# Spreading the first list over layer 0, and pulling rows ahead of pairs in the second product of a four-layer graph network

## Chip, cores and metric

The kernel runs on one NeuronCore of one Trainium2 chip. The metric is the device time of one execution in microseconds (us). In the text PE is TensorE, DVE is VectorE, ACT is ScalarE, POOL is GpSimd and SP is SyncE.

## What is computed

x is 4096 x 128. adj is 4096 x 4096, symmetric in its pattern, with some 0.2% of entries above zero and a full diagonal. There are four layers, each ending in a layer norm of x plus the layer's output.

```python
# layer 0: signed graph attention with the same matrix as mask and weight
hw = x @ W;  scores = where(adj > 0, e_plus[None, :], NEG_INF)
x = layernorm(x + softmax(scores) * adj @ hw)
# layer 1: Chebyshev convolution of order 3, twice (hidden width 256)
Tx1 = L @ x;  Tx2 = 2 * (L @ Tx1) - x
h = elu(x @ W0[0] + Tx1 @ W0[1] + Tx2 @ W0[2] + b0)      # then once more with W1, b1
x = layernorm(x + elu(...))
# layers 2 and 3: attention with four heads, and a mean over neighbours
```

Here L is adj. The change touches layer 0 and the first three of layer 1's four products with L.

## The kernel before

**Dense part.** adj is read from memory as transposed chunks of 512 x 512 in f32 (1 MB each). `chunk` (L145) sends them on SP's queue into a pool of five buffers. There are NB = 8 blocks of IB = 512 rows, each of TB = 4 tiles of 128. A dense product with L goes block by block: for each of 8 chunks `propagate` issues four f32 matmuls into `pacc` (L714), calls a hook `seen`, and at the end of the block the second product forms `t2T` on VectorE (L762), multiplies by W1A (L769), applies ELU (two `hT` on VectorE, L704), and goes on with the next block.

**Sparse part.** Later layers, and part of layer 1, use lists of the entries of each row instead of dense products. For a list, `take` finds in each row of a chunk the 8 largest values and their places (MAX8 and FIND_INDEX8, L1359 and L1360: one pair a row of 128x512). `build(c)` makes list c out of the finds in three steps: the first ends in a `count` (L1386) and, four times over, a chain of MAX8 and MATCH_REPLACE8 (L1398, L1400); the second takes a small matmul with `count` (L1410) and makes `spread` (L1418, L1419); the third takes matmuls with `spread` (L1434) and makes `both_at` (L1462) for lists 0 to 2, or `where` (L1476) for the others. `first_list` (L365) does the takes of list 0 in layer 0.

**Gathers.** GpSimd gathers rows by list with indirect DMAs, each followed by a one-element operation as a pause (L1480, L1526). `pairs(c)` is 36 gathers of both directions of list c's entries (`both_ways`), which need `both_at`. A pull is nine gathers of 128 rows for one unit, that is one tile of 128 rows. In the second product blocks 0 and 1 are done by lists, as units 0 to 7: `pull(u)` gathers, `weigh(u)` makes three `hot` matrices (L1514) and adds six weighed rows to `here` (L1517), and `product(u)` multiplies on TensorE (L1587, L1589). In the third product blocks 0 to 2 are done so, as units 0 to 11 with two buffers for the rows, beside list 3 to 7's building.

**What sets the order.** In layers 0 and 1 a scheduler places the instructions on each engine by its own estimate of when they are ready. `keep_in_program_order` ties an instruction behind the one before it on its engine in the program's text, and to no other. Each engine works through its instructions in the order so fixed. In the second product the plan of hooks (0 to 47, one a chunk) gives the order of the text. Chunks 4 to 7 of a block are FAR: their takes are made in the second product. From the fourth product on the order is written by hand.

In layer 0 the loop goes over i (row block) and n (column chunk); `pos` (L329) makes masks on VectorE, L398 adds up edge sums, L410 the products, `count_bad` (L382) checks each chunk on ScalarE.

Of the kernel before, what the change touches and what calls it, by code (L numbers as in the profile page):

```python
# [11 lines left out]
F32 = mybir.dt.float32  # L12
# [9 lines left out]
P = 128  # L22
# [24 lines left out]
def adj_resnorm_d4(ctx: ExitStack, tc: tile.TileContext, x_in, xT_in, adj, adjT, pairs, diag_in, w0g, w0gT, a0, w1a, b1a,  # L47
# [234 lines left out]
    def layer0(ld, ps_acc, ps_tr, ps_mm):  # L282
# [9 lines left out]
        with tc.tile_pool(name="l0", bufs=1) as l0, tc.tile_pool(name="l0w", bufs=2) as l0w, \  # L292
# [74 lines left out]

            def first_list(i, a):
                top, at = firsts
                for k in range(TB):  # L370
                    row = a[:, k, :]
                    if i == 0:
                        row = x[:, k * TB:(k + 1) * TB, :].rearrange("p t f -> p (t f)")
                        nc.scalar.copy(row, a[:, k, :])
                        d = row[:, k * P:(k + 1) * P]
                        nc.vector.scalar_tensor_tensor(d, ident, less_own[0][:, k:k + 1], d, op0=ALU.mult, op1=ALU.add)
                    nc.vector.max(top[:, k, i, :], row)
                    nc.vector.max_index(at[:, k, i, :], top[:, k, i, :], row)

# [79 lines left out]
            for i in range(2):  # L459
# [5 lines left out]
                for n, j in enumerate(order):  # L465
# [14 lines left out]
                    if j == 0:  # L480
                        first_list(i, a)
                    if n == 1 and rest:
                        diagonal_product(*rest)
                        diagonal_sums(*rest)
# [15 lines left out]
            def sums_of(i, j, pe, first, last, pool=ld, name="chunk"):  # L500
                a = chunk(pool, adjT, i, j, name, True)
                pos = masks(a)
                edge_sums(pe, pos, j, both, first, last)
                count_bad(a, i * NB + j)
                if j == 0:
                    first_list(i, a)
                return j, a, pos
# [5 lines left out]
            for i in range(2, NB):  # L513
# [55 lines left out]
                if i == 5:  # L569
                    tc.keep_in_program_order(nc.sync.dma_start(x, x_in.rearrange("(t p) f -> p t f", p=P)))  # L570
# [91 lines left out]
    degrees, firsts, less_own = [], [], []  # L662

    def network(usual):

        with ExitStack() as whole:
# [3 lines left out]
            with ExitStack() as first, ExitStack() as l1h_pool:  # L670
                ps_acc, ps_tr, ps_mm = [first.enter_context(tc.tile_pool(name=n, bufs=2, space=PSUM, reuse_waits="tile"))
                                        for n in ("ps_acc", "ps_tr", "ps_mm")]
                if usual:
# [4 lines left out]
                    less_own[:] = [early.tile([P, NT], F32, name="less_own")]  # L678
                    nc.scalar.dma_start(own_entries, diag_in)
                    nc.vector.tensor_scalar_mul(less_own[0], own_entries, -1.0)  # L680
# [102 lines left out]
                for ib, blk, p in propagate(lambda jt: t1[:, jt, :], seen=second, blocks=[b for b in range(NB) if not usual or b not in LAST]):  # L783
# [506 lines left out]

    class Lists:
# [3 lines left out]
        def __init__(self, whole, first, layer, own_entries):  # L1295
# [9 lines left out]
            self.diag = own_entries  # L1305
            self.source = keep.tile([P, NT, NEAR + QT], I32, name="source")
# [42 lines left out]
        def take(self, ib, c, a, pinned=False):  # L1349
            pin = tc.keep_in_program_order if pinned else lambda r: r  # L1350
            for k in range(TB):
                t = c * TB + k
                row = a[:, k, :]
                if ib == c:
# [3 lines left out]
                    pin(nc.vector.scalar_tensor_tensor(d, ident, less_own[0][:, t:t + 1], d, op0=ALU.mult, op1=ALU.add))  # L1358
# [3 lines left out]
        def indices(self, out, key):  # L1362

            miss = self.work.tile([P, key.shape[1], key.shape[2]], F32, name=f"miss{key.shape[2]}", bufs=1)
            nc.vector.tensor_scalar(miss, key, 0.0, float(N + 1), op0=ALU.is_le, op1=ALU.mult)
            nc.vector.scalar_tensor_tensor(out, key, -1.0, miss, op0=ALU.add, op1=ALU.add)

        def build(self, c, pinned=False):
            pin = tc.keep_in_program_order if pinned else lambda r: r
            work = self.work  # L1370
# [11 lines left out]
            nc.vector.tensor_scalar(flat(there), flat(top), 0.0, None, op0=ALU.is_gt)  # L1382
            nc.vector.tensor_reduce(deg, rows(there), AX.X, ALU.add)
            nc.vector.tensor_reduce(self.bad[:, 2, c:c + 1], deg, AX.X, ALU.max)
            nc.vector.tensor_scalar(deg, deg, float(-NEAR), 0.0, op0=ALU.add, op1=ALU.max)
            nc.vector.tensor_copy(count, deg)  # L1386
            nc.vector.tensor_copy(flat(key), flat(found_at))
            nc.vector.tensor_tensor(rows(key), rows(key), self.first.rearrange("p s r -> p (s r)")[:, None, :].to_broadcast([P, TB, NB * 8]), ALU.add)
            nc.vector.tensor_mul(flat(key), flat(key), flat(there))
            pairs = top.rearrange("p k s r -> p (k s) r")  # L1390
            nc.vector.tensor_reduce(self.bad[:, 0, c:c + 1], pairs[:, :, 7], AX.X, ALU.max)
            nc.vector.tensor_tensor(twice, pairs[:, :, 0:7], pairs[:, :, 1:8], ALU.is_equal)
            nc.vector.tensor_mul(twice, twice, pairs[:, :, 1:8])
            nc.vector.tensor_reduce(self.bad[:, 1, c:c + 1], twice, AX.XY, ALU.max)
            for k in range(TB):
                row, left = rows(key)[:, k], rows(there)[:, k]
                for n in range(0, MOST, 8):
                    nc.vector.max(best[:, k, n:n + 8], row if n == 0 else left)  # L1398
                    if n + 8 < MOST:
                        nc.vector.match_replace(left, best[:, k, n:n + 8], row if n == 0 else left, -1.0)  # L1400
            nc.vector.tensor_copy(rec[:, :, 0:REST], best[:, :, NEAR:MOST])
            nc.vector.tensor_sub(best[:, :, NEAR:MOST], best[:, :, NEAR:MOST], rec[:, :, 0:REST])
            nc.vector.tensor_copy(rec[:, :, REST:2 * REST], best[:, :, NEAR:MOST])
            nc.vector.tensor_copy(rec[:, :, 2 * REST], self.own.to_broadcast([P, TB]))
# [6 lines left out]
            nc.vector.tensor_copy(base, pb)  # L1411
            nc.vector.tensor_tensor(end, base, deg, ALU.add)
            nc.vector.tensor_copy(rec[:, :, 2 * REST + 1], base)
            nc.vector.tensor_tensor(deg, base, rec[:, :, 2 * REST + 1], ALU.subtract)
            nc.vector.tensor_copy(rec[:, :, 2 * REST + 2], deg)
            at = work.tile([P, TB, SLOTS], BF16, name="spread")
            for k in range(TB):
                nc.vector.tensor_scalar(at[:, k], self.slot, base[:, k:k + 1], None, op0=ALU.is_ge)  # L1418
                nc.vector.scalar_tensor_tensor(at[:, k], self.slot, end[:, k:k + 1], at[:, k], op0=ALU.is_lt, op1=ALU.mult)  # L1419
            nc.scalar.dma_start(self.spread[c], at.rearrange("p k s -> p (k s)"))  # L1420
            nc.vector.tensor_reduce(self.bad[:, 3, c:c + 1], end, AX.X, ALU.max)
            for k in range(TB if c not in PAIRED else 0):
                same = work.tile([P, NEAR, NB * 8], F32, name="same", bufs=1)
                nc.vector.tensor_tensor(same, best[:, k, 0:NEAR][:, :, None].to_broadcast([P, NEAR, NB * 8]),
                                        rows(key)[:, k][:, None, :].to_broadcast([P, NEAR, NB * 8]), ALU.is_equal)
                nc.vector.tensor_tensor(same, same, rows(top)[:, k][:, None, :].to_broadcast([P, NEAR, NB * 8]), ALU.mult)
                nc.vector.tensor_reduce(self.value[:, c * TB + k, QT:], same, AX.X, ALU.add)
            self.indices(self.source[:, ts, QT:], best[:, :, 0:NEAR])
# [13 lines left out]
            nc.vector.tensor_tensor(one(nth), one(self.place), u[:, :, 2 * REST + 1], ALU.subtract)  # L1442
            nc.vector.tensor_tensor(one(nth), one(nth), u[:, :, 2 * REST + 2], ALU.subtract)
            nc.vector.tensor_reduce(entry, u[:, :, 0:2 * REST].rearrange("p j (s k) -> p j k s", s=2), AX.X, ALU.add)
            nc.vector.tensor_tensor(which, self.iota[:, None, 0:REST].to_broadcast([P, n, REST]),
                                    one(nth)[:, :, None].to_broadcast([P, n, REST]), ALU.is_equal)
            nc.vector.tensor_mul(which, which, entry)
            nc.vector.tensor_reduce(one(found), which, AX.X, ALU.add)
            self.indices(self.source[:, ts, 0:QT], found)

            if c in PAIRED:
# [3 lines left out]
                nc.vector.tensor_copy(one(self.into[:, us]), u[:, :, 2 * REST])  # L1455
                nc.vector.tensor_scalar(at, self.source[:, ts], N - 1, 9, op0=ALU.bitwise_and, op1=ALU.logical_shift_left)
                own = work.tile([P, TB, QT], I32, name="high", bufs=1)
                nc.vector.tensor_copy(one(own), u[:, :, 2 * REST])
                nc.vector.tensor_tensor(own, own, self.tile_column, ALU.bitwise_or)
                nc.vector.tensor_tensor(at[:, :, 0:QT], at[:, :, 0:QT], own, ALU.bitwise_or)  # L1460
                nc.vector.tensor_tensor(at[:, :, QT:], at[:, :, QT:], self.column[:, :, None].to_broadcast([P, TB, NEAR]), ALU.bitwise_or)
                nc.vector.tensor_scalar(at, at, n << 21, None, op0=ALU.bitwise_or)  # L1462
# [6 lines left out]
            nc.vector.tensor_copy(source, self.source[:, ts, 0:QT])  # L1469
            nc.vector.tensor_copy(one(where), u[:, :, 2 * REST])  # L1470
            nc.vector.tensor_scalar(where, where, 11, c << 18, op0=ALU.logical_shift_left, op1=ALU.bitwise_or)
            nc.vector.tensor_scalar(high, source, 7 << 9, 12, op0=ALU.bitwise_and, op1=ALU.logical_shift_left)
            nc.vector.tensor_tensor(where, where, high, ALU.bitwise_or)
            nc.vector.tensor_scalar(high, source, IB - 1, None, op0=ALU.bitwise_and)
            nc.vector.tensor_tensor(where, where, high, ALU.bitwise_or)
            nc.vector.tensor_tensor(where, where, self.row, ALU.bitwise_or)  # L1476
# [79 lines left out]
    def second_product(lists, pool, pairs, t1, t1T, xT, hT, v, done, t2_of, second_end):  # L1556
# [6 lines left out]
        got = places[0:2] + places[2:4] * (units // 2 - 1)  # L1563
# [30 lines left out]
        for c, h in ((1, 0), (2, 8)):  # L1594
            build = lists.build(c)
            for n in range(3):
                at(h + 3 * n, next, build)
        at(6, fetch, 1, TB * E)
        at(11, pull, 0)
        at(12, pull, 1)  # L1600
# [519 lines left out]
```

## Time and profile before

| | |
|---|---|
| median of 3 runs | 1674.4 us (1669.16 to 1675.69) |
| the profiled execution, device time | 1672.15 us |
| its span in the profile | 1670.4 us |
| layer 0 | 0 to 350.8 us |
| first product | 350.8 to 577.2 |
| second product | 577.2 to 833.5 |
| third product | 833.5 to 1036.6 |
| fourth product and layers 2 and 3 | 1036.6 to 1670.4 |
| busy: PE, DVE, POOL, ACT | 89%, 66%, 50%, 22% |

All times of instructions come from the one profiled execution, on the clock of its span. A line of a timeline gives the start, the length, the engine, the line of the kernel, the operation, what it writes and reads, and in brackets how long the engine stood idle before it and what it waited for. Busy time of TensorE counts a slow matmul as busy too.

### The profile page before, as it was taken

What the parts mean: (1) busy time and instruction counts of PE and PEld (TensorE: products, weight loads), DVE (VectorE), ACT (ScalarE), POOL (GpSimd) and SP (SyncE); (2) the same over time, 40 slices, a digit from 0 to 9 for tenths busy, and PEclk for the clock granted to TensorE, in tenths of its full rate; (3) what the DMA queues carried; (4) which work ended last, traced back from release to release, by engine and by line L of the source; (5) the groups of instructions that cost most, each with busy time, mean ns of one, the idle gap of its engine ahead of it and who ended that gap; (6) DMA issues with size and microseconds to landing.
All of it is one profiled execution on the core that took longest, in us unless ns stands there. A gap on an engine that the chain in (4) does not pass through costs nothing.

```text
span 1670.4 us, 16412 instructions
## 1 busy us (share of the span) xinstructions
PE 1480.9 (89%) x4744; PEld 719.1 (43%) x4744; DVE 1096.5 (66%) x3204; ACT 374.8 (22%) x690; POOL 835.3 (50%) x1322
## 2 busy tenths in 40 slices
PE   5799999999999999599979899999945788888886
PEld 3344344554444444244434444454423344444444
DVE  4887554788979696977669622255435766656676
ACT  5575450110000011112200000022223111122234
POOL 0000000000234048848768878888727888888851
PEclk9899999999999999799989899999976788889998
DMA  9776775578798977476568878988846667778773
GB/s 346 301 292 252 277 251 209 193 250 307 286 345 307 310 267 265 144 262 218 197 236 287 277 252 284 328 297 286 294 106 186 196 205 239 243 239 264 250 190 104
DMA packets 106972, 419.30 MB, mean 251 GB/s; under 512 B 21556, under 2 KB 44088, under 8 KB 67064
## 3 DMA queue, kind: packets, MB, share of 16 engines
q1 hardware_dynamic: 59984, 360.01, 60.4%
q0 software_dynamic: 22656, 36.17, 8.6%
q10 hardware_dynamic: 24232, 21.98, 4.4%
q8 instruction: 39, 0.64, 0.2%
q14 instruction: 61, 0.50, 0.1%
HBM read 404.39 MB, written 13.70 MB: 250 GB/s over the span
## 4 chain that ended last, share of the span: by engine, by line
PE 50%; DVE 20%; POOL 12%; DMA 9%; issue 6%; ACT 3%; SPq 1%; ACTq 0%; DVEq 0%; POOLq 0%
PE pacc L714 19%; PE pacc L410 11%; PE pp L2013 7%; POOL got L1783 5%; DMA got<-table,source 5%; DVE at L1360 3%; POOL got L1480 3%; DVE top L1359 2%; PE pp L1894 2%; POOL both_ways L1480 2%; DMA got<-rows,source 2%; POOL idle L1526 2%; DVE gw L1819 2%; DVE acc L1907 2%; DMA chunk<-in_adjT 1%
## 5 line engine op out<-in xcount | busy, mean ns | idle before, releaser
L1783 POOL DMA_INDIRECT got<-table,source x288 | 275.8, 958 | 88.3 <-issue 61.6
L1894 PE MATMUL pp<-chunk,xT 128*128 128x512 f32 x496 | 245.5, 637 | 1.0 <-ACT xT L1865 0.7
L714 PE MATMUL pacc<-chunk,x 128*128 128x512 f32 x512 | 222.6, 593 | 0.0
L1480 POOL DMA_INDIRECT got<-rows,source x180 | 181.4, 1008 | 56.6 <-issue 27.1
L410 PE MATMUL pacc<-chunk,hw 128*128 128x512 f32 x408 | 192.1, 616 | 0.2
L1328 POOL IOTA i<- 128x384 int32 (+3 forms) x4 | 0.9, 238 | 360.7 <-PE pden L398 345.0
L2013 PE MATMUL pp<-chunk,w 128*128 128x512 f32 x384 | 170.2, 592 | 0.0
L714 PE MATMUL pacc<-chunk,t 128*128 128x512 f32 x384 | 170.0, 593 | 0.0
L714 PEld LDWEIGHTS pacc<-chunk,x 128*128 128x128 f32 x512 | 96.0, 190 | 114.9 <-issue 114.9
L714 PE MATMUL pacc<-chunk,v 128*128 128x512 f32 x320 | 144.9, 604 | 0.0
L1480 POOL DMA_INDIRECT both_ways<-in_pairs,both_at x108 | 106.7, 988 | 72.7 <-DVE both_at L1462 55.5
L1359 DVE MAX8 top<-chunk 128x8 f32<-128x512 f32 x196 | 128.4, 677 | 17.6 <-DMA chunk<-in_adjT 17.6
L1894 PEld LDWEIGHTS pp<-chunk,xT 128*128 128x128 f32 x496 | 95.4, 205 | 91.6 <-issue 85.8
L1360 DVE FIND_INDEX8 at<-top,chunk 128x8 uint16<-128x512 f32 x196 | 133.0, 684 | 0.0
L410 PEld LDWEIGHTS pacc<-chunk,hw 128*128 128x128 f32 x408 | 76.6, 196 | 93.7 <-issue 90.1
L1526 POOL TENSOR_TENSOR idle<-idle 128x1 f32<-128x1 f32 x489 | 111.2, 227 | 8.5
L1517 DVE SCALAR_TENSOR_TENSOR here<-got,back,here 128x128 f32<-128x128 f32 x120 | 42.2, 351 | 100.9 <-DMA got<-rows,source 98.7
L714 PEld LDWEIGHTS pacc<-chunk,t 128*128 128x128 f32 x384 | 71.1, 190 | 81.0 <-issue 81.0
L329 DVE TENSOR_SCALAR pos<-chunk 128x2048 bf16<-128x2048 f32 x66 | 80.2, 1220 | 37.5 <-DMA chunk<-in_adjT 29.8
L382 ACT ACTIVATE junk<-chunk 128x2048 fp8e4<-128x2048 f32 x51 | 97.4, 1910 | 32.9 <-DMA chunk<-in_adjT 32.2
L2013 PEld LDWEIGHTS pp<-chunk,w 128*128 128x128 f32 x384 | 70.5, 190 | 76.5 <-issue 76.5
L714 PEld LDWEIGHTS pacc<-chunk,v 128*128 128x128 f32 x320 | 60.5, 194 | 78.2 <-issue 78.2
(381 smaller groups left out, 2021.1 us busy)
## 6 DMA issues: line engine op xcount, KB each, us to landing
chunk<-in_adjT SPq DMA_DIRECT2D x326, 1024.0 KB, 5.9
keep<-in_adjT SPq DMA_DIRECT2D x13, 1024.0 KB, 8.3
spread<-spread ACTq DMA_DIRECT2D x16, 384.0 KB, 3.5
got<-table,source POOLq DMA_INDIRECT x288
chunk<-in_adjT ACTq DMA_DIRECT2D x4, 1024.0 KB
got<-rows,source POOLq DMA_INDIRECT x180
table<-rows ACTq DMA_DIRECT2D x8, 264.0 KB, 6.7
xT<-in_xT ACTq DMA_DIRECT2D x8, 256.0 KB, 6.7
```

The source lines that it names most:

```text
L329: r = nc.vector.tensor_scalar(pos, a, 0.0, None, op0=ALU.is_gt)
L382: nc.scalar.activation(junk, a, AF.Relu, scale=-1.0, accum_out=bad[:, n:n + 1], saturate=False)
L410: in_order(nc.tensor.matmul(p, hw[:, j * TB + k, :], a[:, k, :], start=first and k == 0, stop=last and k == TB - 1))
L714: nc.tensor.matmul(p, stationary(c * TB + k), a[:, k, :], start=n == 0 and k == 0, stop=n == NB - 1 and k == TB - 1)
L1359: pin(nc.vector.max(self.top[:, t, ib, :], row))
L1360: pin(nc.vector.max_index(self.at[:, t - TB, ib, :], self.top[:, t, ib, :], row))
L1480: tc.keep_in_program_order(nc.gpsimd.indirect_dma_start(out, None, of, bass.IndirectOffsetOnAxis(ap=index, axis=0)))
L1517: r = nc.vector.scalar_tensor_tensor(here, got[:, j, 0:F], self.back[:, u, j:j + 1], here, op0=ALU.mult, op1=ALU.add)
L1526: return nc.gpsimd.tensor_tensor(self.idle[:, 0:1], of, self.idle[:, 1:2], ALU.mult)
L1783: nc.gpsimd.indirect_dma_start(got[t][:, j, :], None, table, bass.IndirectOffsetOnAxis(ap=lists.source[:, t, j:j + 1], axis=0))
L1894: nc.tensor.matmul(p, y[:, t0 + k, :], a[:, ib % (TB // n), k, :], start=k == 0, stop=k == n - 1)
L2013: nc.tensor.matmul(p, w[:, c * TB + k, :], a[:, k, :], start=n == 0 and k == 0, stop=n == NB - 1 and k == TB - 1)
```

## The change

Six things are edited.

1. `first_list`: for i below 7 one ScalarE copy of the whole chunk goes into a half of x (unused there until layer 0 ends), and its four takes are queued; one is done after each later chunk. At i = 7 all four are done at once.
2. The diagonal of the copied rows is cleared by (ident == 0) * row in place of adding -diag * ident; the operation that made -diag is gone, and the load of `diag` stands later on ScalarE's queue.
3. The load of x is issued at i = 7 in place of i = 5.
4. The second product goes through the chunks of a block in the order 0, 4, 1, 5, 2, 6, 3, 7, so that each second one is FAR.
5. The plan of hooks: pulls 0 and 1 are first, ahead of list 1's pairs; other pulls, weighs and products move; list 2 is built at hooks 14, 17, 20 in place of 8, 11, 14; list 2's 36 pairs are fetched at hook 35 in place of 9 at 17 and 27 at 40. Units 2 and 3 now also take their rows into hT.
6. In `build(c, True)` each VectorE instruction is tied to the one before it. Lists 1 to 7 are built so; list 0 is not.

```diff
             def first_list(i, a):
                 top, at = firsts
-                for k in range(TB):
-                    row = a[:, k, :]
+                rows = a
+                if i < NB - 1:
+                    while takes:
+                        takes.popleft()()
+                    rows = x[:, i % 2 * (NT // 2):(i % 2 + 1) * (NT // 2), :].rearrange("p (k t) f -> p k (t f)", k=TB)
+                    nc.scalar.copy(rows, a)
+                def take(k):
+                    row = rows[:, k, :]
                     if i == 0:
-                        row = x[:, k * TB:(k + 1) * TB, :].rearrange("p t f -> p (t f)")
-                        nc.scalar.copy(row, a[:, k, :])
                         d = row[:, k * P:(k + 1) * P]
-                        nc.vector.scalar_tensor_tensor(d, ident, less_own[0][:, k:k + 1], d, op0=ALU.mult, op1=ALU.add)
+                        nc.vector.scalar_tensor_tensor(d, ident, 0.0, d, op0=ALU.is_equal, op1=ALU.mult)
                     nc.vector.max(top[:, k, i, :], row)
                     nc.vector.max_index(at[:, k, i, :], top[:, k, i, :], row)
+                for k in range(TB):
+                    takes.append(lambda k=k: take(k))
+                if i == NB - 1:
+                    while takes:
+                        takes.popleft()()
...
                     if j == 0:
                         first_list(i, a)
+                    elif takes and i and n > 1:
+                        takes.popleft()()
...
                 if j == 0:
                     first_list(i, a)
+                elif takes:
+                    takes.popleft()()
...
-                if i == 5:
+                if i == 7:
                     tc.keep_in_program_order(nc.sync.dma_start(x, x_in.rearrange("(t p) f -> p t f", p=P)))
...
-                    less_own[:] = [early.tile([P, NT], F32, name="less_own")]
-                    nc.scalar.dma_start(own_entries, diag_in)
-                    nc.vector.tensor_scalar_mul(less_own[0], own_entries, -1.0)
...
-                for ib, blk, p in propagate(lambda jt: t1[:, jt, :], seen=second, blocks=[b for b in range(NB) if not usual or b not in LAST]):
+                for ib, blk, p in propagate(lambda jt: t1[:, jt, :], order=[0, 4, 1, 5, 2, 6, 3, 7], seen=second, blocks=[b for b in range(NB) if not usual or b not in LAST]):
...
+    class in_order_engine:
+        def __init__(self, engine, pin):
+            self.engine, self.pin = engine, pin
+        def __getattr__(self, name):
+            call = getattr(self.engine, name)
+            return lambda *a, **kw: self.pin(call(*a, **kw))
...
+            nc.scalar.dma_start(self.diag, diag_in)
...
         def build(self, c, pinned=False):
             pin = tc.keep_in_program_order if pinned else lambda r: r
+            vector = in_order_engine(nc.vector, pin)
...
-            nc.vector.tensor_scalar(flat(there), flat(top), 0.0, None, op0=ALU.is_gt)
+            vector.tensor_scalar(flat(there), flat(top), 0.0, None, op0=ALU.is_gt)
...
-        got = places[0:2] + places[2:4] * (units // 2 - 1)
+        got = places[0:2] * 2 + places[2:4] * 2
...
-        for c, h in ((1, 0), (2, 8)):
-            build = lists.build(c)
+        for c, h in ((1, 0), (2, 14)):
+            build = lists.build(c, True)
             for n in range(3):
                 at(h + 3 * n, next, build)
-        at(6, fetch, 1, TB * E)
-        at(11, pull, 0)
-        at(12, pull, 1)
-        at(17, fetch, 2, 9)
-        at(18, lists.paired, 0)
-        at(30, lists.paired, 1)
-        for u, h in enumerate((20, 24, 28, 32, 33, 37, 40, 41)):
+        for u, h in ((0, 0), (1, 0), (2, 12), (3, 14), (4, 25), (5, 25), (6, 31), (7, 34)):
+            at(h, pull, u)
+        at(7, fetch, 1, TB * E)
+        at(9, lists.paired, 0)
+        at(27, lists.paired, 1)
+        for u, h in enumerate((10, 12, 24, 25, 29, 32, 34, 37)):
             at(h, weigh, u)
             at(h + 1, product, u)
-        for u, h in ((2, 25), (3, 25), (4, 29), (5, 33), (6, 34), (7, 38)):
-            at(h, pull, u)
-        at(40, fetch, 2, TB * E)
+        at(35, fetch, 2, TB * E)
```

## The prediction

> **What bounds the kernel now.** I read the slices of the span first, then a table by stage, then TensorE's waits in each stage, then the timeline of the engine that each wait names.
>
> ```profile
> core 0: us, PE busy (x) PEld busy (x) DVE busy (x) ACT busy (x) POOL busy (x), PEclk, DMA share, GB/s
> 0.00:350.80 350.80, 317.06 (x1238) 144.08 (x1239) 228.23 (x545) 149.09 (x173) 1.50 (x11) 0.96 0.71 263
> ...
> 577.20:833.50 256.30, 232.42 (x687) 111.23 (x686) 194.13 (x567) 43.28 (x75) 175.99 (x288) 0.97 0.67 228
> 833.50:1036.60 203.10, 186.45 (x594) 91.42 (x593) 120.51 (x515) 14.87 (x31) 159.91 (x251) 0.95 0.79 267
> ```
>
> The columns are the stretch, its length, and the busy time of PE, PEld, DVE, ACT and POOL. The stages that the diff touches are layer 0 (first line), the second product and the third product. TensorE is busy in each for all but 34, 24 and 17 us: only those waits, and the slower clock after them, are to be had. The first product (350.8 to 577.2) is full.
>
> Layer 0's waits of TensorE:
>
> ```profile
> PE pmm L348 <- DMA A<-in_a: 9.1, 1, 9.1
> PE pden L398 <- DVE pos L329: 9.0, 7, 2.9
> PE ptr L405 <- DVE parts L445: 4.6, 1, 4.6
> ```
>
> Columns: total, times, longest. The first is the start. The others are VectorE being late, and the first list's block of eight takes stands before them.
>
> The second product's waits, and VectorE and GpSimd at that place:
>
> ```profile
> PE pmm L769 <- DVE t2T L762: 19.8, 5, 16.6
> PE ptr L774 <- DVE hT L704: 2.7, 5, 1.2
> ```
>
> ```profile
> 643.00 0.68 DVE L762 SCALAR_TENSOR_TENSOR t2T<-pacc,xT 128x512 f32<-128x512 f32 x1
> ...
> 666.61 0.35 DVE L1517 SCALAR_TENSOR_TENSOR here<-hT,back,here 128x128 f32<-128x128 f32 x1 [14.30 <-DMA hT<-rows,source]
> 668.83 0.35 DVE L1517 SCALAR_TENSOR_TENSOR here<-hT,back,here 128x128 f32<-128x128 f32 x1 [1.61 <-DMA hT<-rows,source]
> ...
> 671.49 0.40 DVE L1517 SCALAR_TENSOR_TENSOR here<-hT,back,here 128x128 f32<-128x128 f32 x1 [0.36 <-DMA hT<-rows,source]
> ...
> 697.56 0.67 DVE L762 SCALAR_TENSOR_TENSOR t2T<-pacc,xT 128x512 f32<-128x512 f32 x1
> ```
>
> ```profile
> 607.24 0.97 POOL L1480 DMA_INDIRECT both_ways<-in_pairs,both_at  x1 [55.47 <-DVE both_at L1462]
> ...
> 658.03 0.97 POOL L1480 DMA_INDIRECT hT<-rows,source  x1 [0.15 <-issue]
> ```
>
> GpSimd starts the 36 pair gathers of list 1 at 607.24, only then unit 0's rows (658.03). VectorE stands still 14.3 us in front of unit 0's first `here`, then owes takes; the block's `t2T` comes at 697.56 and TensorE has waited 16.6 us. Note the price: from the start of the pair gathers to the sixth `here` of a unit pulled behind them it is 671.49 - 607.24 = **64.3 us**.
>
> The third product has the same pattern:
>
> ```profile
> 855.50 0.35 DVE L1517 SCALAR_TENSOR_TENSOR here<-got,back,here 128x128 f32<-128x128 f32 x1 [7.03 <-DMA got<-rows,source]
> ...
> 858.77 0.35 DVE L1517 SCALAR_TENSOR_TENSOR here<-got,back,here 128x128 f32<-128x128 f32 x1 [2.75 <-DMA got<-rows,source]
> ...
> 863.37 0.16 DVE L1386 CAST count<-degree 128x4 bf16<-128x4 f32 x1
> ```
>
> ```profile
> 863.58 0.16 PE L1410 MATMUL u<-count,below 128*128 128x4 bf16 x1 [7.91 <-DVE count L1386]
> ```
>
> Only three of unit 0's six `here` stand before list 4's count, and TensorE already waits 7.9 us for that count. Later GpSimd's gathers set the end: 108 row gathers and 12 value gathers in 182 us.
>
> **What the skill says.** The page "PSUM — Partial Sum Buffer", section "Engine vs sequencer instructions", says that VectorE's queue is strict FIFO. The trace agrees: nothing of VectorE ran in the 14.3 us. "Perfetto Trace Analysis", section "DMA Instruction — SWDGE (GPSIMD)", says that the shown end of such a gather is the end of descriptor writing, not of the data. Here too: the fourth gather of unit 0 began at 662.07, took 0.97 us, and its `here` ran at 666.61, 4.5 us after the start. "TensorE: Matmul & The Clock Gate", section "What's actually happening", says an idle window of about 3.4 us halves TensorE's clock; the page's PEclk row shows 7 (0.7 of full speed) in the slice that holds the 16.6 us wait, which agrees as far as a mean over 42 us can. So a wait that goes also returns part of a clock loss.
>
> **The change, part by part.** The order of the instructions on each engine tells more here than the plan of hooks, so I read it for both kernels.
>
> *Layer 0, gain.* The takes (0.68 + 0.68 us a row) are as many as before, but now one after each later chunk, from a copy that ScalarE makes (six more copies of 128x2048 in sum, about 1.9 us each by `count_bad`'s 1.91; ScalarE is at 149 of 351 us). Gone: the 4.6 us wait for `parts`; VectorE's 3.5 us wait for the `diag` DMA at 21.6 (the product with less_own is gone, and diag is sent from ACT's queue after the first count); some 6 of the 11.9 us for `pos` (L398, L341); and about 5 us of slow clock after these (four L405 transposes took 1.87 against 0.95 later). That is 19. Back come 0 to 3 us because the 2 MB load of x (7.6 us at the stage's 263 GB/s) moves on SP's queue from 165.4, where SP then stood 8.2 us for a `keep` buffer anyway, to just before the last chunks; it still has over 50 us until x is read at about 299. And about 3 come back where single takes delay a mask. Sum **-13**, ends -18 and -4.
>
> *Second product, loss.* Pulls 0 and 1 do go ahead of the pair gathers on GpSimd's queue: 18 gathers, one each 1.355 us with its pause (658.03 to 659.37), are 24.4 us from about 582, so units 0 and 1 no longer wait. But pull 2 and 3 stand behind the 36 pair gathers, and unit 2's six `here` (hook 24 of the plan) are in VectorE's order before the second block's `t2T` (hook 15): only the `here` are tied to the one before, the three `hot` ahead of them are not, so the group floated up. The time of it: list 1's first step, serial now, no longer lies in the first product but after 579.4: 12 small operations 3.8, four rows x 1.2, four casts 0.8, about 10 with the links between; two FAR chunks 2 x 5.44 = 10.9; spread step 4.5; one chunk 5.4; `t2T` 0.7; last step 3.6. So both_at is ready at 614.5, against 607. Plus 64.3 gives the sixth `here` of unit 2, and `t2T`, at 679. TensorE gets there at 610 + 36.8 (the spacing 606.2 to 643.0) + 2 x 0.87 = 648.5: a **wait of 30 us**. Before it some 3.5 us for list 1's spread and the first `t2T`, after it 2.7 for list 2's spread (VectorE has 37.4 us of work in a block of 36.8), and 0 to 4 for the rest. The old stage without its waits is 256.3 - 23.6 = 232.7; with the new ones 269 to 273. **+15**; ends +3 (the group waits for fewer gathers, alternate chunks shorten the tail) and +24 (slow clock).
>
> *Third product, loss.* List 3's first step, formerly done early in the second product, now stands here, and all lists are tied in order. In VectorE's order all twelve `here` of units 0 and 1 come before list 4's count, all of units 2 and 3 before list 5's; list 3's last spread stands behind unit 0's fifth `here`. With the old times of the gathers: spread of list 3 at 860 (TensorE wanted it at 848), count 4 after unit 1's last gather (870.83 + 5) at about 877 instead of 863.4, its spread at 891, product 0 at 893 (884.65). The `where` of list 3 comes at 881, so twelve value gathers end at 898, pull 2 at 911, pull 3 at 924, landed 929. Count 5, before ready at 880.6, comes at 929.5, TensorE wants it at 909: 20 us. Product 2 follows at 948 (918.84). Its two buffers hold pull 4 back, so GpSimd idles from 924 to 948 and its eight pulls behind it end as much later: 29 less a few of the 7.4 us that it waited later. **+26**, ends +6 and +33.
>
> *Nothing:* is_equal in place of the less_own multiply (same operation, 0.35 us, in the same places; VectorE has 36 us free a stage), and everything after 1036.6, where the hand order is unchanged; were it hit, the difference would be a pull or two.
>
> Sum: -13 + 15 + 26 = +28 on the profiled execution's own 1672.15, so **1700**. That execution is 2.2 under the median of 1674.4, which I leave in the range.
>
> **Rivals.**
> A. *It works as named.* The gathers come early enough, alternate takes (5.44 in 6.88 us of TensorE) keep `t2T` on time: second product -21, third 0, layer 0 -13: 1638. For it: those are the waits shown. Against: the pairs still stand between pulls 1 and 2.
> B. *Second product cured, third product hit*: -13 - 18 + 26: 1667. It decides if unit 2's `here` finds its rows by 648, which needs both_at 30 us earlier than I have it.
> C. *Second product hit, third not*, GpSimd's chain hiding the late counts: -13 + 15 + 3: 1677. It needs product 2 before about 922, so that pull 4 follows pull 3.
> D. *Layer 0 gives nothing* (VectorE's sum is the same, x late): 1713.
> My own forecast is the mechanism "`here` behind a late gather"; it decides as soon as a unit's `here` stands before a `t2T` or count that TensorE wants earlier than gather + 4.5 us.
>
> **Chances.** Mine 0.56, A 0.08, B 0.12, C 0.14, D 0.10. About 0.5% (8.4 us) is what a measurement can tell from no change: faster means below 1666, slower above 1682.8. A and some of B are faster, 0.12; B's rest, part of C and mine's low end are same, 0.14; slower 0.74. The range 1672 to 1718 leaves out A, part of B, and the sums beyond D.
>
> **What would show it.** Right: TensorE waits about 30 us for `t2T` near 650 to 680 and VectorE waits as long for hT rows; in the third product a wait of some 20 us for count, with GpSimd idle before pull 4; layer 0 ends near 338. Wrong: no wait over 10 us for `t2T`, or a third product of 203 us or less.

## The result, and the profile after

| | before | after |
|---|---|---|
| median | 1673.8 us (6 runs) | 1721.3 us (6 runs, 1717.3 to 1724.3) |
| span of the profiled execution | 1670.4 | 1721.5 |
| layer 0 | 350.9 | 335.9 |
| first product | 226.3 | 226.3 |
| second product | 256.3 | 277.6 |
| third product | 203.6 | 246.6 |
| the rest | 633.3 | 635.1 |

The ratio is 1.0286 (95% interval 1.0264 to 1.0307): slower by 47.6 us. A ratio leaves out executions more than 1.5% slower than the fastest of their kernel, so it can differ from the ratio of the medians. In the tables of this part a stage runs from its first matmul with a chunk to that of the next, and the third product to 0.9 us after the start of the last matmul with `wd`. Five of the later runs fell on occasions on which the kernel before took 1829 to 1848 us itself; they are compared only with what ran beside them.

The table by stage, after (columns as before):

```profile
0.00:335.90 335.90, 310.75 (x1235) 140.89 (x1240) 227.67 (x544) 159.10 (x176) 1.50 (x11) 0.98 0.74 275
...
562.20:839.80 277.60, 235.66 (x687) 112.78 (x686) 200.50 (x563) 45.99 (x79) 175.51 (x288) 0.93 0.62 215
839.80:1086.10 246.30, 192.23 (x595) 93.82 (x594) 140.87 (x570) 13.17 (x27) 156.15 (x251) 0.89 0.64 216
```

Layer 0 gained 15: TensorE is idle there for 25 us instead of 34, and busy for 311 instead of 317, with a mean clock of 0.98 in place of 0.96. The second product lost 21 and the third 43. TensorE has the same work in them (687 matmul records in the second as before, 595 after 594 in the third) but is idle for 42 and 54 us, where it was 24 and 17. Its busy time grew by only 3 and 6 us. GpSimd is no busier, VectorE by 6 and 20 us (list 3's first step is part of that; it has moved into the third product). So most of the time went into waits.

TensorE's waits after, in the second product and then in the third:

```profile
PE pmm L783 <- DVE t2T L776: 38.5, 3, 33.7
```

```profile
PE u L1435 <- DVE count L1312: 28.1, 2, 17.1
PE u L1459 <- DVE spread L1312: 18.1, 4, 9.9
PE ptr L154 <- ACT t2T L819: 7.2, 1, 7.2
```

(The lines have moved: L776 was L762, L783 L769, L1435 L1410, L1459 L1434, L1505 L1480, L1542 L1517, L1667 L1645. VectorE's instructions of a tied list all carry L1312.)

GpSimd, VectorE and TensorE around the 33.7 us:

```profile
599.80 0.97 POOL L1505 DMA_INDIRECT both_ways<-in_pairs,both_at  x1 [5.24 <-DVE both_at L1312]
```

```profile
656.45 0.35 DVE L1542 SCALAR_TENSOR_TENSOR here<-hT,back,here 128x128 f32<-128x128 f32 x1 [31.03 <-DMA hT<-rows,source]
...
665.73 0.35 DVE L1542 SCALAR_TENSOR_TENSOR here<-hT,back,here 128x128 f32<-128x128 f32 x1 [2.22 <-DMA hT<-rows,source]
666.30 0.68 DVE L776 SCALAR_TENSOR_TENSOR t2T<-pacc,xT 128x512 f32<-128x512 f32 x1
```

```profile
667.04 2.08 PE L783 MATMUL pmm<-t2T,W1A 128*128 128x512 f32 x2 [33.74 <-DVE t2T L776]
```

Read them from the top. The pair gathers start at 599.80, 37.6 us into the stage (the prediction had 614.5 - 577.2 = 37.3). Unit 2's rows stand behind them, from 649.72 on. VectorE comes to the first of its `here` at 625.4, stands still for 31 us, runs the sixth at 665.73, and then `t2T`. From the pairs' start to the start of the sixth it is 65.9 us, against the 64.3 read from before. VectorE had free time here, and `t2T` could have been made some 33 us earlier; it only stood behind `here`.

In the third product the largest wait, and then GpSimd's waits for a buffer:

```profile
936.36 0.16 PE L1435 MATMUL u<-count,below 128*128 128x4 bf16 x1 [17.10 <-DVE count L1312]
```

```profile
957.80 0.97 POOL L1505 DMA_INDIRECT got<-rows,source  x1 [23.53 <-PE ptr L1667]
...
980.58 0.97 POOL L1505 DMA_INDIRECT got<-rows,source  x1 [10.64 <-PE ptr L1667]
...
1054.67 0.97 POOL L1505 DMA_INDIRECT got<-rows,source  x1 [5.64 <-PE ptr L1667]
```

List 5's count comes at 936, product 2 at 956.7 (116.9 us into the stage; 85.3 before), and pull 4 waits for it with both buffers full. The other two lines are pull 5, which waits for product 3, and pull 10, which waits for product 8. Before, pulls 4 and 10 had no such wait:

```profile
921.49 0.97 POOL L1480 DMA_INDIRECT got<-rows,source  x1 [0.15 <-issue]
...
1004.43 0.97 POOL L1480 DMA_INDIRECT got<-rows,source  x1 [0.32 <-PE ptr L1645]
```

From the start of the stage, pull 4 starts 30.0 us later than before, pull 5 40.5, pull 7 37.2, pull 8 38.6 and pull 10 43.9; the end of pull 11 is 43.8 later. So the third product's 43 us are those of GpSimd's chain, which is held back for products 2, 3 and 8.

### The profile page after: what moved, and what is told of

The parts are those of the page before. It is cut to its first block, busy times and chain, and to the rows that moved or that the text cites. A ratio compares the mean times of both kernels' runs of the same rounds, so it can differ in the third digit from the quotient of the medians.

```text
span 1721.5 us, 16411 instructions
## 1 busy us (share of the span) xinstructions
PE 1480.6 (86%) x4740; PEld 718.8 (42%) x4744; DVE 1115.0 (65%) x3203; ACT 385.6 (22%) x693; POOL 832.7 (48%) x1322
## 4 chain that ended last, share of the span: by engine, by line
PE 52%; DVE 16%; POOL 16%; DMA 8%; issue 6%; ACT 3%; ACTq 0%; DVEq 0%; POOLq 0%
PE pacc L728 18%; PE pacc L423 12%; PE pp L2035 7%; POOL got L1805 5%; POOL got L1505 5%; DMA got<-table,source 4%; PE pp L1916 3%; POOL idle L1551 3%; POOL both_ways L1505 2%; DMA got<-rows,source 2%; DVE at L1384 2%; DVE top L1383 1%; DVE gw L1841 1%; PE pmm L783 1%; DVE acc L1929 1%
## 5 line engine op out<-in xcount | busy, mean ns | idle before, releaser
L1916 PE MATMUL pp<-chunk,xT 128*128 128x512 f32 x496 | 242.0, 629 | 1.0 <-ACT xT L1887 0.7
L1505 POOL DMA_INDIRECT got<-rows,source x180 | 180.7, 1004 | 99.4 <-PE ptr L1667 39.8
L728 PE MATMUL pacc<-chunk,v 128*128 128x512 f32 x320 | 149.2, 618 | 0.0
L1542 DVE SCALAR_TENSOR_TENSOR here<-got,back,here 128x128 f32<-128x128 f32 x120 | 41.8, 351 | 122.1 <-DMA got<-rows,source 119.4
L1505 POOL DMA_INDIRECT both_ways<-in_pairs,both_at x108 | 105.8, 979 | 22.5 <-issue 17.1
L329 DVE TENSOR_SCALAR pos<-chunk 128x2048 bf16<-128x2048 f32 x66 | 80.1, 1219 | 33.5 <-DMA chunk<-in_adjT 31.6
```

Source lines behind the costliest of these rows:

```text
L329: r = nc.vector.tensor_scalar(pos, a, 0.0, None, op0=ALU.is_gt)
L728: nc.tensor.matmul(p, stationary(c * TB + k), a[:, k, :], start=n == 0 and k == 0, stop=n == NB - 1 and k == TB - 1)
L1505: tc.keep_in_program_order(nc.gpsimd.indirect_dma_start(out, None, of, bass.IndirectOffsetOnAxis(ap=index, axis=0)))
L1542: r = nc.vector.scalar_tensor_tensor(here, got[:, j, 0:F], self.back[:, u, j:j + 1], here, op0=ALU.mult, op1=ALU.add)
L1916: nc.tensor.matmul(p, y[:, t0 + k, :], a[:, ib % (TB // n), k, :], start=k == 0, stop=k == n - 1)
```

## The experiments

**Stages of the kernels run.** Each number comes from one profile.

| kernel | median us | layer 0 | second | third | rest |
|---|---|---|---|---|---|
| before | 1673.8 | 350.9 | 256.3 | 203.6 | 633.3 |
| after | 1721.3 | 335.9 | 277.6 | 246.6 | 635.1 |
| e1 hots tied | 1662.2 | 335.0 | 242.3 | 216.4 | 640.8 |
| e2 lists 3 to 7 untied | 1678.7 | 335.3 | 276.9 | 203.4 | 633.8 |
| e3 edits 1 to 3 alone | 1659.0 | 335.6 | 255.5 | 207.8 | 637.2 |
| e4 edit 6 alone | 1709.9 | 350.9 | 253.7 | 245.7 | 636.3 |
| e5 both cures | 1643.1 | 336.6 | 242.3 | 204.6 | 633.3 |
| e6 e5, chunks 0 to 7 | 1641.9 | 335.5 | 240.5 | 203.3 | 635.1 |
| e7 before, pulls 0, 1 first | 1656.4 | 350.8 | 239.1 | 204.9 | 633.3 |
| e8 pairs behind pulls | 1689.7 | 334.6 | 249.2 | 244.0 | 632.5 |
| e9 edits 1 to 3 and pulls first | 1642.8 | 335.4 | 239.2 | 204.9 | 633.6 |

The theory throughout: a unit's `here` stands on VectorE ahead of a `t2T` or a list's count or spread that TensorE wants earlier than the unit's rows can land. The rival: tied lists, or the new plan, are slow in themselves.

**e1_hots_tied.** The changed kernel, with

```diff
             for j in range(QT):
-                nc.vector.tensor_scalar(hot[:, j, :], ...)
+                r = nc.vector.tensor_scalar(hot[:, j, :], ...)
+                if pinned:
+                    tc.keep_in_program_order(r)
```

> The changed kernel, and in weigh the three `hot` are tied to the instruction before them as the six `here` are, so that a unit's group stays where the plan puts it: unit 2's behind the second block's t2T, units 0 and 1 of the third product behind the counts of lists 3 to 5. Theory 1 (`here` behind late gathers, put ahead of what TensorE waits for): the 33.7 us wait for t2T goes and the second product takes 240 to 246 in place of 277.6; the third takes 198 to 212 in place of 246.3; in all about 1645. Rival (tied lists are slow in themselves, their serial chains hold count and spread back): the second product improves, the third stays at 235 or more; about 1685.

Measured: 1662.2 us, 0.9937 of before (0.9921 to 0.9954). The order of instructions shows unit 2's group behind the third `t2T` of the stage, and the counts of lists 3 to 5 ahead of unit 0's. The largest of TensorE's waits in the second product, and that for `t2T`, are then:

```profile
PE u L1614 <- DVE here L1544: 4.1, 5, 1.7
PE pmm L783 <- DVE t2T L776: 1.8, 3, 1.2
```

The 33.7 us are gone with three ties and no other edit: 277.6 became 242.3. In the third product 30 of the 43 went. 13 stayed: TensorE now waits 11.4 us there for gathered rows themselves, which in the kernel before it did not; why this order brings that was not tested. The theory holds in both places, against the rival's 235 or more; the total missed the expected 1645 by those 13 and by some in the rest.

**e2_untied_third.** The changed kernel, with

```diff
-            vector = in_order_engine(nc.vector, pin)
+            vector = in_order_engine(nc.vector, pin) if c < 3 else nc.vector
```

> The changed kernel, but lists 3 to 7 (built in the third product) are not tied; lists 1 and 2 are. Theory 1: `here` and counts of the third product stand as in the kernel before (three `here` of unit 0 ahead of list 4's count), so it takes about 204; the second product keeps unit 2's `here` ahead of the second t2T and stays at about 278; in all about 1679. Rival (the third product is long because its gathers and list 3 start late after the new second product): the third stays at 235 or more, 1710 or more.

Measured: 1678.7 us, 1.0037 (1.0019 to 1.0056). The third product is back at 203.4, though it starts as late as in the changed kernel; the second keeps its wait (33.5 us for `t2T`). Without the tie of its lists the third product loses nothing, wherever it starts. That the tie is not slow in itself is e1's result: there the lists stay tied, and 30 of the 43 us go.

**e3_layer0_only.** Edits 4 to 6 undone.

> Edits 1 to 3 alone (first list spread, diagonal by is_equal, x load at i = 7); second and third product and the lists as before. If layer 0's 15.0 us are a gain of its own: about 1659, layer 0 at 336 and the second and third product at 256 and 203. Rival (what is won there is lost again in the second product, where the gathers then start no earlier): 1665 to 1674.

Measured: 1659.0 us, 0.9914 (0.9895 to 0.9932). Layer 0's 15 us are its own; in the median nothing takes them back.

**e4_tie_only.** The kernel before with `in_order_engine` in `build`; lists 1 and 2 are built untied as there.

> The kernel before with edit 6 alone, for lists 3 to 7 (lists 1 and 2 were built untied and stay so). Theory 1: the third product gets the order of `here` and counts of the changed kernel and takes about 246, second product within 10 us of before; in all about 1715. Rival (the tie costs little, the loss of the third product comes with the new second product): 1675 to 1688.

Measured: 1709.9 us, 1.0216 (1.0195 to 1.0237); third product 245.7. So edit 6 alone makes 42 of the third product's 43 us.

**e5_tied_second_only.** e1's tie in the second product only, and e2's edit.

> The changed kernel with both cures: in the second product the three `hot` of a unit are tied as its `here` are, and lists 3 to 7 are not tied. If the two losses are separate and add up: layer 0 335, first product 226, second 242 (as with the hots tied), third 203 (as with lists 3 to 7 untied), the rest 634 to 638: about 1643, below both kernels. Rival (the third product needs list 3's first step early, which the new second product has no room for): the third 212 or more, 1652 or more.

Measured: 1643.1 us, 0.9821 (0.9799 to 0.9844). The two losses are separate and add up, and without them the change is faster than the kernel before.

**e6_same_natural_order.** e5 without edit 4:

```diff
-propagate(lambda jt: t1[:, jt, :], order=[0, 4, 1, 5, 2, 6, 3, 7], seen=second, ...)
+propagate(lambda jt: t1[:, jt, :], seen=second, ...)
```

> As e5_tied_second_only, but the second product goes through the chunks in the order 0 to 7. What alternating is worth by itself: four chunks with takes in a row are 21.8 us of VectorE against 13.8 of TensorE, so t2T may come up to 8 us late in a block where list or unit work stands behind them. Expected 4 to 12 us more in the second product, 1647 to 1655. Rival (alternating gives nothing, VectorE catches up in the four chunks without takes): within 3 us of e5_tied_second_only.

Measured: 1641.9 us, 0.9817 (0.9789 to 0.9844). My expectation was wrong: alternating chunks gives nothing here. TensorE waits for `t2T` 3.2 us in sum, no more than 2.5 at once. That fits the rival's reason, that VectorE catches up in the four chunks without takes.

**e7_pulls_first_only.** The kernel before, with

```diff
+        at(0, pull, 0)
+        at(0, pull, 1)
         at(6, fetch, 1, TB * E)
-        at(11, pull, 0)
-        at(12, pull, 1)
```

> The kernel before with one edit of the plan: pulls 0 and 1 stand at hook 0 in place of 11 and 12, so ahead of list 1's pairs on GpSimd. Theory 1: VectorE's 14.3 us in front of unit 0's `here` go, the 16.6 us wait for t2T with them, and some of the slow clock: second product 235 to 241 in place of 256, in all about 1656. Rival (the backlog of takes makes t2T late anyway): second product 250 or more, 1668 or more.

Measured: 1656.4 us, 0.9901 (0.9876 to 0.9926). The second product takes 239.1, as little as with the whole new plan mended (242.3 in e5, 240.5 in e6), from two lines of the plan. Its first gather starts at 583.84, after a wait of 32 us for the stored rows of t1, in time that GpSimd had free.

**e8_pairs_behind_pulls.** The changed kernel, with

```diff
-        at(7, fetch, 1, TB * E)
+        at(14, fetch, 1, TB * E)
```

> The changed kernel with list 1's 36 pairs moved from hook 7 to hook 14, behind pulls 2 and 3 on GpSimd; unit 2's `here` stay ahead of the second t2T in VectorE's order. Theory 1: unit 2's rows land near 632, where TensorE wants t2T at 633, so the 33.7 us wait shrinks to 0 to 6; second product 242 to 252; the third stays at 246; about 1690. Rival (the pairs, now late, hold unit 4 and those behind it back): second product 262 or more.

Measured: 1689.7 us, 1.0105 (1.0081 to 1.013); second product 249.2. The order on VectorE is still the bad one, but the rows come in time, and TensorE waits no more than 3.9 us for a `t2T`. What counts is the pair of an early place in one queue and a late place in the other.

**e9_layer0_and_pulls.** Edits 1 to 3 and e7's.

> Edits 1 to 3 and, of the plan, only pulls 0 and 1 moved to hook 0; no tie of lists, chunks in the order 0 to 7, the other hooks as before. If everything that the change won comes from layer 0 (15 us) and these two pulls (17 us), it takes 1641 to 1643, the same as with the whole plan mended; if moving the other hooks, tying lists 1 and 2 and alternating chunks gave something of their own, it takes 1648 or more.

Measured: 1642.8 us, 0.9821 (0.9797 to 0.9845), the same as e5 and e6 within their spread. So the rest of the plan, the ties and the alternation add nothing to these four edits. It is the simplest of the kernels near 1642.

**e10_diag_only and e11_x_late_only.** The kernel before with edit 2 alone, and with edit 3 alone (`if i == 5` to `if i == 7`).

> The kernel before with edit 2 alone: the diagonal cleared by is_equal, no less_own, the load of diag behind the first count on ScalarE's queue. As predicted, VectorE's 3.5 us wait at 21.6 goes and its lateness up to 90 us with it: 2 to 5 us less, about 1670. Rival (first masks wait for their chunks anyway, the wait is hidden): 0 to 1 less.

> The kernel before with edit 3 alone: the load of x at i = 7. If it shared the DMA engines with what TensorE needed at 165 to 190: up to 3 us less. If its new place delays the last chunks: 0 to 3 us more. Predicted near nothing alone: 1671 to 1675; then most of layer 0's 15 us belong to the spread takes.

Measured: 0.9975 (0.9965 to 0.9985), 4.4 us less, and 0.9969 (0.9959 to 0.9979), 5.5 us less. The second is a miss: I had near nothing. The mask of a `keep` chunk in VectorE's timeline, first before, then in e11:

```profile
180.81 1.23 DVE L329 TENSOR_SCALAR pos<-keep 128x2048 bf16<-128x2048 f32 x1 [3.25 <-DMA keep<-in_adjT]
```

```profile
174.45 1.23 DVE L329 TENSOR_SCALAR pos<-keep 128x2048 bf16<-128x2048 f32 x1 [1.67 <-DMA keep<-in_adjT]
```

With x in front of it, the chunk that SP sends next had its mask some 6.4 us later, and its DMA took SP 8.23 us to issue, where e11 shows 0.42. TensorE's 2.9 us wait at 188 to 191 and one of 0.7 behind it are not there in e11. The eight matmuls after them took 5.40 us before and 3.70 in e11. In sum that is 5.3 us, and the stage became 5.0 shorter.

**e12 to e22: the third product's other 17 us.** The changed kernel with only unit 4's `hot` tied in the third product, which puts list 6's spread ahead of unit 4's `here`:

```diff
-            lists.weigh(u, v[:, tile_of(u), :], got[u], here, hot, True)
+            lists.weigh(u, v[:, tile_of(u), :], got[u], here, hot, 2 if u == 4 else True)
```

with `if pinned == 2` around the tie of e1.

> The changed kernel with one unit's three `hot` tied in the third product, unit 4's, so that list 6's spread stands ahead of unit 4's `here` on VectorE. The third product took 17 us more than predicted. If these come from a third turn of the same mechanism (list 6's spread behind unit 4's rows, TensorE's 9.9 us wait, product 3 and GpSimd's second wait for a buffer behind it): the third product takes 229 to 238 in place of 246.6, in all about 1709. Rival (GpSimd's late gathers alone set the rest, list 6's spread is hidden): 243 or more, 1718 or more.

Measured: 1853.6 us, with 1848.3 for the kernel before on that occasion; layer 0 and first product had their usual 335.8 and 226.3, the second product 322.8. Nothing from the second product on can be compared with the table. Again:

> The kernel of e12_unit4_tied once more, on another occasion, since there the kernel before took 1848 us and every stage with gathers was longer. Third turn of the mechanism at list 6: third product 229 to 238, about 1709. Rival: 243 or more, 1718 or more.

Measured: 1849.2 us, 1840.1 for the kernel before: as little use. Then with the changed kernel beside it:

> The changed kernel itself, as the control for e15_unit4_tied_beside on the same occasion. Where the kernel before takes 1673: 1721; where it takes some 1845: some 3% more than that.

> Unit 4's three `hot` tied, beside the control. Third turn of the mechanism at list 6: third product 9 to 17 us shorter than in the control, TensorE's 9.9 us wait for spread before product 3 gone, 10 to 14 us less in all. Rival (GpSimd's late gathers alone set the rest): within 4 us of the control.

Measured: 1718.1 and 1712.7 us (kernel before: 1673.3), third product 243.1 and 236.7. TensorE's wait for list 6's spread, 9.8 us in the control, is down to 1.3:

```profile
967.88 0.24 PE L1459 MATMUL u<-rec,spread 128*128 128x39 bf16 x3 [1.32 <-DVE spread L1312]
```

Product 3 comes at 970.0 in place of 976.5. So there is a third turn of the mechanism, worth 6.4 us in the stage and 5.4 in all, less than the 9 to 17 and 10 to 14 that I expected. The next suspect was ScalarE's queue. After the change it reads, with TensorE's matmul that waits for it:

```profile
1042.78 0.40 ACT L1537 ACTIVATE here<-v,diag 128x128 f32<-128x128 f32 x1 [16.46 <-DVE hot L1539]
...
1043.55 0.59 ACT L819 COPY t2T<-pacc 128x512 f32<-128x512 f32 x1
```

```profile
1044.19 1.12 PE L154 MATMUL ptr<-ident,t2T 128*128 128x128 f32 x4 [7.20 <-ACT t2T L819]
```

A unit's first step (L1537) stood ahead of the copy that TensorE wanted, and waited 16.5 us for VectorE. The next kernel is e15's with that step tied too, in the third product:

```diff
-            nc.scalar.activation(here, own, AF.Copy, ...)
+            r = nc.scalar.activation(here, own, AF.Copy, ...)
+            if tie_act:
+                tc.keep_in_program_order(r)
```

> As e15_unit4_tied_beside (changed kernel, unit 4's hot tied), and in the third product ScalarE's first step of each `here` (own row times diag, L1537) is tied to the instruction before it, so that it no longer stands ahead of ScalarE's copy t2T (L819), for which TensorE waited 8.5 us at 1034. If this queue accounts for the rest of the third product's loss: that wait goes, the third product takes 226 to 232 in place of 236.7, the whole 6 to 9 us less than e15, about 1705. Rival (the copy is hidden behind GpSimd's late gathers): within 3 us of e15, 1710 or more.

Measured: 1815.0 us, 1828.5 for the kernel before there: 0.9987 (0.9957 to 1.0016). Then beside its control (e17 to e20 have no measurement):

> The kernel of e16_act_tied_too beside that of e15 on one occasion. ScalarE's queue as a cause: 6 to 9 us less than e22_unit4_control, at 1673 for the kernel before about 1705. Rival: within 3 us of it.

> The kernel of e15, as the control: about 1712 where the kernel before takes 1673, and 1.005 of the kernel before where that takes some 1840.

Measured: 1839.3 and 1851.0 us (kernel before 1846.0): 0.9979 (0.995 to 1.0008) against 1.0039 (1.0018 to 1.006). The third product takes 238.5 against 250.2, 11.7 less. But this is not the price of the wait for the copy. That wait was 8.8 us in e22 (the trace names ScalarE's instruction just ahead of the copy), and in e21 most of it is still there:

```profile
PE ptr L154 <- ACT t2T L819: 5.8, 1, 5.8
```

Two other things differ. One is VectorE's order. In e22 the counts of lists 4 and 5 come 50.1 and 95.6 us into the stage, behind all `here` of units 0 and 1, and of 2 and 3. In e21 they come at 30.1 and 64.5, list 4's ahead of unit 0's `here`, list 5's ahead of unit 1's. Product 2 follows at 91.7 us in place of 116.6. So with a tie on ScalarE's queue the scheduler placed whole groups on VectorE's queue elsewhere, which takes away part of the first two turns. The other is that in e22 TensorE stands 11.4 us near the end of the stage for nothing that the profile shows, and in e21 it does not. The 11.7 us cannot be divided between these, and what ScalarE's order costs by itself was not measured.

## Why the prediction was right in kind and too small

The direction, the mechanism and both places were right; the size was not. 51.1 us were added to the span where 28 were forecast, and 1721.3 lies 3 us above the range.

- **Layer 0, -13 forecast, -15.0 measured.** Right in sum, wrong in its parts, so that the sum came near in part by luck. The step "Back come 0 to 3 us", for the move of x's load, had the wrong sign: the old place cost 5.5 us by itself (e11), because x stood on SP's queue in front of a chunk whose mask came 6.4 us late. I had read SP's 8.2 us at that chunk as a wait for a buffer that would be there anyway; in e11 they are gone. The diag term, 3.5, measured 4.4 alone (e10). If the three edits add up, 15 - 4.4 - 5.5 leaves some 5 for the spread takes, which were not run alone; I had given them and the clock 15 before deductions.
- **Second product, +15 forecast, +21.3 measured.** The steps hold: the pairs' start 37.6 us into the stage (37.3 forecast), 65.9 for the group (64.3), a wait of 33.7 (30). e1, e5 and e8 show each in its own way that this wait is the loss. Mis-sized were the 3.7 us on the wait itself and the clock after it: TensorE's busy time rose from 232.4 to 235.7 with the same matmuls, the clock from 0.97 down to 0.93, for which the sum had no term and only the upper end a mention.
- **Third product, +26 forecast, +43 measured.** This is where the range broke. Product 2 was forecast at 948 - 833.5 = 114.5 us into the stage and came at 116.9. List 3's spread, list 5's count and pull 4's wait were as worked out; list 4's count came 6.6 us later than that, product 0 3.1. The step that failed is "its eight pulls behind it end as much later: 29 less a few of the 7.4". It has GpSimd run freely from pull 4 on and puts all later waits at nothing. Pull 4 is 30.0 us later than before, and 3.8 came back at pull 7, as forecast; but 10.5 were added at pull 5 and 5.3 at pull 10. I had stopped reading the order at list 5. List 6's spread stands behind unit 4's rows in the same way and holds product 3 and pull 5; that turn alone, taken away, gives 6.4 us (e15 against e14). Ahead of product 8 and pull 10 stands TensorE's 7.2 us wait for ScalarE's copy t2T, with a unit's first step ahead of that copy. That this wait makes pull 10's 5.3 us is read from the trace and was not shown by a run: e16 and e21 changed VectorE's order as well. In e14, the changed kernel once more, the wait for the copy is 4.9, GpSimd's wait before pull 10 3.1 in place of 5.6, and the third product 243.1 in place of 246.6, so two profiles of one kernel differ here by 3.5 us.
- **The rest, 0 forecast, +1.8 measured**, within what one profile of a kernel differs from another (632 to 641 in the table).
- **Rivals.** A, "it works as named", is what e5 shows once the two orders are mended (1643 where it said 1638), so the intention was sound and its order on VectorE was not. Its alternate takes have no part in that: in e6 `t2T` is on time without them. B and C, each with one place cured, are e8 (1690 where B said 1667, with the third product's full 43) and e2 (1679 where C said 1677): the places are independent.

## What to carry to other kernels

Where a scheduler fills an in-order queue, look up for each operand that comes by a slow gather what stands behind its reader on the reader's engine. Compare the landing time with when the next engine wants the first of those. Do so for every turn of the loop and on every engine that touches the unit, not just for the first two turns. A tie that holds only the last instructions of a group does not hold the group: its untied first ones float up and the tied ones with them. A tie on one engine can move the groups of another, so read the order of all engines again after each edit, before a difference is put down to it. Before a plan of many hooks is rewritten, try the one move that the wait names; here two pulls put first gave the second product's whole 17 us.

## What was not expected of the hardware

On the occasions on which the kernel before took 1829 to 1848 us, layer 0 and the first product took their usual 336 and 226 us in all five profiles. In e12 the second product took 323 in place of 277 and the rest 728 in place of 635. So only the stages from the second product on were longer, and yet a gather kept its 0.97 us on GpSimd. The traces of these occasions have waits for nothing that the profile shows, or for something outside it. In the second and third product of e22 TensorE stands 28 us in such waits, VectorE 49 and ScalarE 77; in e15, the same kernel at 1712.7 us, none of the three has one. What they wait for is open. And a 2 MB load that nobody awaited for 130 us cost 5.5 us through the one chunk queued behind it.
